# Zero-filled rows and columns for the products of layer 2 of a four-layer convolution and scan network

## Chip, cores and metric

The kernel runs on one core of a Trainium2 chip. The metric is the device time of one execution in microseconds (us). Several executions were timed, and the median is compared. A profile of one execution was taken with the hardware profiler; all its times count from the start of its span.

## The reference, cut to what matters

The network takes four images of 64 channels and 64 x 64 pixels, all float32, through four layers. Layers 0 and 3 are state-space scans with convolutions and a norm around them, and layer 1 is a larger scan in two directions. The change is in layer 2. As the kernel carries it out, layer 2 computes this for every pixel:

- a 3 x 3 convolution from 64 to 32 channels, with a bias;
- a leaky rectifier, the larger of `0.2 * h` and `h`;
- a 1 x 1 convolution from 32 channels to 9 values, with a bias, and a softmax over the 9 values, which gives a 3 x 3 filter of its own for each pixel;
- the filtered image: the sum over the 9 neighbours of filter value times pixel, the same filter for all 64 channels;
- twice the pixel minus the filtered image, which goes to layer 3.

## The kernel before, in words

`image` runs the four layers one after the other for each of the four images. A compile-time scheduler orders the instructions of each engine; each engine then runs its own list in order and waits for semaphores. Only layer 1 has its order written out by hand (`in_order`). In layer 2 the list is what the scheduler makes of the calls at the end of `layer2` (L1066 to L1071): `weights(c + 1)` is issued ahead of `filtered(c)`, and `turned(c + 1)` behind it.

The image lies in `x2` with a border of zeros, twice: the upper half of the rows is read from partitions 0 to 63 (the channels), and a copy made at L984 puts the lower half on partitions 64 to 127. So one chunk `c` covers 512 pixels of the upper half and 512 of the lower half, and there are four chunks per image.

For each chunk:

- `weights` makes the filters. For each of the 9 taps and each half it issues one product (L1008, recorded at the helper line L158): 64 rows of the array (the channels of that half), 32 columns (the hidden channels), 512 moving columns (pixels). The two halves use different rows and different columns of the array and write partitions 0 to 31 and 32 to 63 of `p1`. ScalarE adds the bias (L1013, tile `h1` of 64 x 512), and VectorE applies the rectifier (L1014). Four second products (L1017) take `h1` as the stationary side, 64 rows by 128 pixels, with the 18 columns of `l2_w2` moving. VectorE and ScalarE make the softmax (L1024 to L1033).
- `turned` transposes the filters (L1040), so that 18 rows (two halves of 9 taps) by 512 pixels result, and ScalarE copies them from PSUM to `wT` (L1045).
- `filtered` spreads each tap. For tap k a product with the one-hot matrix `pick[:, k]` (18 rows, 128 columns) and `wT` (18 rows, 512 moving columns) copies the filter value of a pixel to all 64 channels of its half, into `pk` (L1056, four PSUM buffers). VectorE multiplies `pk` by the shifted image to `m` (L1058, four buffers), and GpSimd subtracts `m` from the accumulator `acc` (L1060, for eight taps). The accumulator starts as twice the pixel (L1053). For the last tap GpSimd writes the result of each half to `x3` (L1064).

A float32 product is recorded as two matmuls and two weight loads. One 3 x 3 convolution of a chunk is thus 36 records, in 18 pairs of one record for each half, and the nine spreads are 18 records.

Layer 3 begins with `mamba_front`: the products `d_pc` and `d_pz` (64 rows, 128 columns) read `x3`, and the copy `d_xb` (L394) fills a constant. `setup` loads all constants once, those of layer 2 at L212 to L221, on the SyncE queue.

Of the kernel before, what the change touches and what calls it, by code (L numbers as in the profile page):

```python
# [10 lines left out]
F32 = mybir.dt.float32  # L11
AF = mybir.ActivationFunctionType
# [7 lines left out]
NB, C, H, W = 4, 64, 64, 64  # L20
HW = H * W
TOK = 512
# [43 lines left out]
class Net:  # L66
# [94 lines left out]
    def setup(self, sp, pp):  # L161
        nc = self.nc
        self.use_exp()
        self.unscale = self.ctile([128, 1], "unscale")
        nc.vector.memset(self.unscale, -23.0 * math.log(2.0))
        self.shift = self.ctile([128, 1], "shift")
        nc.vector.memset(self.shift, -SHIFT)
        self.ln_half = self.ctile([128, 1], "ln_half")
        nc.vector.memset(self.ln_half, -math.log(2.0))
        self.ln_eps = self.ctile([128, 1], "ln_eps")  # L170
        nc.vector.memset(self.ln_eps, LN_EPS)
        self.ident = ident = self.ctile([128, 128], "ident")
        make_identity(nc, ident)


        self.tri_in = ti = self.ctile([128, 128], "tri_in")
        nc.gpsimd.memset(ti, 1.0)
        nc.gpsimd.affine_select(
            out=ti, in_=ti, compare_op=ALU.is_ge, fill=0.0, base=0,
            pattern=[[1, 128]], channel_multiplier=-1,  # L180
        )
        nc.gpsimd.memset(ti[0:64, 64:128], 0.0)
        self.tri_after = ta = self.ctile([128, 128], "tri_after")
        nc.gpsimd.memset(ta, 1.0)
        nc.gpsimd.affine_select(
            out=ta, in_=ta, compare_op=ALU.is_ge, fill=0.0, base=-1,
            pattern=[[-1, 128]], channel_multiplier=1,
        )
        nc.gpsimd.memset(ta[64:128, 0:64], 0.0)

        self.tri2 = t2 = self.ctile([128, 64], "tri2")
        nc.vector.tensor_tensor(t2, ti[:, 0:64], ti[:, 64:128], ALU.add)
        self.ident2 = i2 = self.ctile([128, 64], "ident2")
        nc.vector.tensor_tensor(i2, ident[:, 0:64], ident[:, 64:128], ALU.add)
        nc.vector.tensor_scalar(i2, i2, math.exp(SHIFT - LN_EPS), None, ALU.mult)

        self.mask48 = m48 = self.ctile([64 + GC, GC], "mask48")
        nc.vector.tensor_tensor(
            m48, ident[0 : 64 + GC, 0:GC], ident[0 : 64 + GC, 64 : 64 + GC], ALU.add
        )  # L200

        self.mean64 = self.ctile([C, C], "mean64")
        nc.vector.memset(self.mean64, 1.0 / C)
        self.cen64 = self.ctile([C, C], "cen64")
        nc.vector.tensor_tensor(self.cen64, ident[0:C, 0:C], self.mean64, ALU.subtract)

        self.setup_l0(sp, pp)
        self.l1 = [self.setup_l1(sp, pp, d) for d in "wh"]
        self.l1_beta = self.ctile([C, 1], "l1_beta")
        nc.vector.tensor_tensor(self.l1_beta, self.l1[0]["beta"], self.l1[1]["beta"], ALU.add)  # L210

        self.l2_w1 = self.ctile([2 * C, 9, 32], "l2_w1")  # L212
        self.l2_b1 = self.ctile([C, 1], "l2_b1")
        self.l2_w2 = self.ctile([C, 2, 9], "l2_w2")
        nc.vector.memset(self.l2_w2, 0.0)
        self.l2_b2 = self.ctile([128, 9], "l2_b2")
        nc.sync.dma_start(self.l2_b2, self.a["l2_b2"].to_broadcast([128, 9]))
        for h in range(2):
            nc.sync.dma_start(self.l2_w1[h * C : (h + 1) * C], self.a["l2_w1"])
            nc.sync.dma_start(self.l2_b1[32 * h : 32 * h + 32], self.a["l2_b1"])  # L220
            nc.sync.dma_start(self.l2_w2[32 * h : 32 * h + 32, h], self.a["l2_w2"])  # L221
        self.setup_l3(sp, pp)

    def bn_scale(self, out_s, out_b, g, b, m, v):
# [753 lines left out]
    def layer2(self, b, x2):  # L978


        nc, tc = self.nc, self.tc
# [3 lines left out]
        with ExitStack() as ctx:  # L985
            sp = ctx.enter_context(tc.tile_pool(name=f"c{b}_s", bufs=2))
            ps = ctx.enter_context(tc.tile_pool(name=f"c{b}_ps", bufs=4, space=PSUM))
            pb = ctx.enter_context(tc.tile_pool(name=f"c{b}_pb", bufs=4, space=PSUM))
            rows = lambda x: x.rearrange("p (r w) -> p r w", w=W)
            pick = sp.tile([18, 9, 2 * C], F32, name=f"pick{b}", tag="pick", bufs=1)  # L990
            for h in range(2):
                nc.vector.tensor_copy(
                    pick[:, :, h * C : (h + 1) * C],
                    self.ident[0:18, 9 * h : 9 * h + 9].unsqueeze(2).to_broadcast([18, 9, C]),
                )

            def view(c, k):
                r = c * ROWS + k // 3
                return x2[:, r : r + ROWS, k % 3 : k % 3 + W]

            def weights(c):

                n = f"c{b}_{c}"
                p1 = ps.tile([128, TOK], F32, name=f"{n}_p1", tag="ps")
                for k in range(9):
                    for h in range(2):
                        P = slice(h * C, (h + 1) * C)
                        self.mm(  # L1008
                            p1[32 * h : 32 * h + 32], self.l2_w1[P, k, :], view(c, k)[P],
                            k == 0, k == 8,  # L1010
                        )
                h1 = sp.tile([C, TOK], F32, name=f"{n}_h1", tag="h1")
                nc.scalar.activation(h1, p1[0:C], AF.Identity, bias=self.l2_b1)  # L1013
                nc.vector.scalar_tensor_tensor(h1, h1, 0.2, h1, ALU.mult, ALU.max)  # L1014
                p2 = ps.tile([128, TOK], F32, name=f"{n}_p2", tag="ps")
                for j in range(4):
                    self.mm(  # L1017
                        p2[:, 18 * j : 18 * j + 18], h1[:, 128 * j : 128 * j + 128],
                        self.l2_w2.rearrange("p h k -> p (h k)"),
                    )  # L1020
                wl = sp.tile([128, 8, 9], F32, name=f"{n}_wl", tag="wl")
                st = sp.tile([128, 8], F32, name=f"{n}_st", tag="st")
                wide = st.unsqueeze(2).to_broadcast([128, 8, 9])
                nc.vector.tensor_tensor(  # L1024
                    wl, p2[:, 0:72].rearrange("p (j k) -> p j k", k=9),
                    self.l2_b2.unsqueeze(1).to_broadcast([128, 8, 9]), ALU.add,
                )
                nc.vector.tensor_reduce(st, wl, AX.X, ALU.max)
                nc.vector.tensor_tensor(wl, wl, wide, ALU.subtract)
                nc.scalar.activation(wl, wl, AF.Exp)  # L1030
                nc.vector.tensor_reduce(st, wl, AX.X, ALU.add)
                nc.vector.reciprocal(st, st)
                nc.vector.tensor_tensor(wl, wl, wide, ALU.mult)  # L1033
                return wl

            def turned(c, wl):
                n = f"c{b}_{c}"
                p3 = ps.tile([128, TOK], F32, name=f"{n}_p3", tag="ps")
                for j in range(4):
                    nc.tensor.transpose(  # L1040
                        p3[0:18, 128 * j : 128 * j + 128],
                        wl[:, 2 * j : 2 * j + 2, :].rearrange("p h k -> p (h k)"), self.ident,
                    )
                wT = sp.tile([18, TOK], F32, name=f"{n}_wT", tag="wT")
                nc.scalar.copy(wT, p3[0:18])  # L1045
                return wT

            def filtered(c, wT):
# [12 lines left out]
                for h in range(2):  # L1061
                    P = slice(h * C, (h + 1) * C)
                    t0 = 3 + c * TOK + h * HW // 2
                    nc.gpsimd.tensor_tensor(x3[:, t0 : t0 + TOK], acc[P], m[P], ALU.subtract)  # L1064

            wT = turned(0, weights(0))  # L1066
            for c in range(NCH // 2):
                wl = weights(c + 1) if c + 1 < NCH // 2 else None
                filtered(c, wT)
                if wl is not None:  # L1070
                    wT = turned(c + 1, wl)  # L1071
# [80 lines left out]
```

## Time and profile before

| | |
|---|---|
| median of 3 runs | 20212.52 us (20205.84 to 20241.59) |
| profiled execution, its own time | 20241.61 us |
| its span in the profile | 20239.9 us |
| mean granted TensorE clock | 0.952 |
| layer 2 of the first image, first convolution record to the last write of `x3` | 4470.6 to about 4581.1 us |
| the 3 x 3 convolutions start in the other images at | 9509.1, 14564.8 and 19610.1 us |

The profile lists for each group of instructions the source line, the engine, the operation, the tile written and the tiles read, the shape and the number of records. `PE` is TensorE's matmul and `PEld` its weight load; `DVE` is VectorE, `ACT` ScalarE, `POOL` GpSimd and `SP` SyncE. `18*128 18x512` on a matmul means 18 rows and 128 columns of the array and 512 moving columns. Tile names are given with the numbers left out: `c_p` stands for p1, p2 and p3 of layer 2, `c_pk` for the spread filters, `c_m` for the products on VectorE, `c_acc` for the accumulator, `c_h` for h1; names with `d_` belong to layer 3, and `x` written at L1064 is `x3`. The granted clock is the share of TensorE's full clock that its throttle let through. Matmuls are pipelined and a record's length holds its latency, so the pace of a stream is read from the distance between starts.

### The profile page before, as it was taken

To read this page: it belongs to the slowest core of one execution; us is meant where nothing else is said; L and a number is where in the kernel's file an instruction comes from. 1 tells how busy PE (TensorE), PEld (TensorE's weight loads), DVE (VectorE), ACT (ScalarE), POOL (GpSimd) and SP (SyncE) were. 2 spreads that over 40 slices of the span, in tenths; PEclk is the share of its full clock that TensorE was granted. 3 is DMA by queue.
4 is the path that set the end of the run, shared out by engine and by line. 5 is a ranking of instruction groups with operands and counts; after the bars stand their busy time and mean duration, and the time that the engine had idled before them with its cause. 6 is when DMAs were issued, how large, how long until landed. Compare 5 with 4: busy or idle time off the path is not lost. (4 is left out here: it accounts for less than half of the span.)

```text
span 20239.9 us, 622630 instructions
## 1 busy us (share of the span) xinstructions
PE 18436.4 (91%) x269256; PEld 11821.8 (58%) x269256; DVE 16728.8 (83%) x20282; ACT 12294.7 (61%) x15342; POOL 10582.6 (52%) x8660
## 2 busy tenths in 40 slices
PE   7899999997799999999789999999977999999997
PEld 2666666662266666666226666666622666666652
DVE  7888878878888888887988888888798888788879
ACT  3577667763367766775336776777533677667753
POOL 4555545555555555555555554555555555455555
PEclk9999999998899999999889999999988999999998
DMA  0233333320023333332002333333200233333320
GB/s 6 64 82 82 81 77 81 81 70 4 1 67 83 83 77 80 81 82 66 4 1 70 83 82 75 81 81 82 65 4 1 72 83 82 75 81 81 83 63 2
DMA packets 558931, 1264.96 MB, mean 62 GB/s; under 512 B 159416, under 2 KB 160800, under 8 KB 556192
## 3 DMA queue, kind: packets, MB, share of 16 engines
q1 hardware_dynamic: 556192, 1225.12, 24.6%
q8 instruction: 2124, 34.80, 0.7%
q14 instruction: 615, 5.04, 0.1%
HBM read 6.24 MB, written 4.19 MB: 1 GB/s over the span
## 5 line engine op out<-in xcount | busy, mean ns | idle before, releaser
L857 ACT ACTIVATE b_k_e<-b_z,shift 128x768 f32<-128x768 f32 x6144 | 5532.2, 900 | 4474.7 <-PE b_z L158 3718.5
L865 POOL TENSOR_TENSOR b_k_tB<-b_BC,tri 128x512 f32<-128x512 f32 x3072 | 3437.7, 1119 | 7431.7 <-PE b_u_S L158 6664.8
L903 DVE TENSOR_TENSOR b_k_r<-b_u_S,b_k_r 128x768 f32<-128x768 f32 x6144 | 5860.2, 954 | 977.6 <-DMA b_k_r<-b_k_r 262.2
L880 DVE TENSOR_TENSOR b_k_e<-b_k_e,b_wt 128x768 f32<-128x768 f32 x6144 | 6176.4, 1005 | 29.2 <-ACT b_k_e L857 29.2
L158 PE MATMUL b_u_S<-b_k_e,b_k_tB 64*64 64x192 f32 x98304 | 5425.8, 335 | 583.8 <-DVE b_k_r L903 491.8
L857 ACT ACTIVATE b_k_r<-b_z,ln_eps 128x768 f32<-128x768 f32 x6144 | 5488.7, 893 | 0.0
L158 PE MATMUL b_y<-b_k_r,b_k_dC 64*64 64x192 f32 x98304 | 5192.2, 323 | 64.0 <-ACT b_yt L923 61.3
L158 PE MATMUL b_z<-A,b_T 48*64 48x384 f32 x49152 | 5215.4, 487 | 4.3 <-ACT b_k_r L857 4.1
L158 PEld LDWEIGHTS b_y<-b_k_r,b_k_dC 64*64 64x64 f32 x98304 | 3915.9, 133 | 2171.8 <-issue 1489.2
L865 POOL TENSOR_TENSOR b_k_dC<-b_BC,ident 128x512 f32<-128x512 f32 x3072 | 4755.9, 1548 | 3.3 <-DMA b_BC<-b_BC 1.9
L158 PEld LDWEIGHTS b_u_S<-b_k_e,b_k_tB 64*64 64x64 f32 x98304 | 3278.3, 132 | 1851.9 <-DVE b_k_r L903 1015.2
L158 PEld LDWEIGHTS b_z<-A,b_T 48*64 48x64 f32 x49152 | 1913.5, 134 | 225.5 <-DVE b_yg L772 57.8
L438 ACT ACTIVATE d_a<-d_dl,l_A 128x512 f32<-128x512 f32 x512 | 368.7, 721 | 1089.8 <-DVE d_h L443 1089.8
L438 ACT ACTIVATE a_a<-a_dl,l_A 128x512 f32<-128x512 f32 x512 | 367.9, 720 | 1052.1 <-DVE a_h L443 911.6
L447 POOL TENSOR_TENSOR a_y<-a_y,a_o 128x512 f32<-128x512 f32 x512 | 821.1, 1604 | 287.9 <-DVE a_o L446 274.0
L447 POOL TENSOR_TENSOR d_y<-d_y,d_o 128x512 f32<-128x512 f32 x512 | 758.8, 1482 | 221.8 <-DVE d_o L446 208.5
L158 PE MATMUL a_pq<-a_sl,a_xb 128*128 128x512 f32 x1024 | 626.2, 696 | 262.1 <-DVE a_o L446 151.7
L158 PE MATMUL d_pq<-d_sl,d_xb 128*128 128x512 f32 x1024 | 643.9, 715 | 232.3 <-DVE d_o L446 185.1
L158 PE MATMUL d_pb<-d_sl,d_xb 128*128 128x512 f32 x1024 | 650.3, 722 | 180.8 <-DVE d_o L446 177.6
L443 DVE TENSOR_TENSOR_SCAN d_h<-d_a,l_state,d_g 128x512 f32<-128x512 f32 x512 | 738.2, 1458 | 5.4
L443 DVE TENSOR_TENSOR_SCAN a_h<-a_a,l_state,a_g 128x512 f32<-128x512 f32 x512 | 697.9, 1365 | 17.2 <-ACT a_a L438 9.8
L158 PE MATMUL a_pb<-a_sl,a_xb 128*128 128x512 f32 x1024 | 605.9, 677 | 41.2 <-DVE a_o L446 38.1
(343 smaller groups left out, 12651.5 us busy)
## 6 DMA issues: line engine op xcount, KB each, us to landing
b_k_r<-b_k_r SPq DMA_DIRECT2D x6144, 192.0 KB, 3.0
b_BC<-b_BC SPq DMA_DIRECT2D x512, 12.0 KB, 1.9
xin<-in_x SPq DMA_DIRECT2D x16, 256.0 KB, 6.0
out<-d_so SPq DMA_DIRECT2D x32, 128.0 KB, 2.3
l1w_cw<-in_l1w_cw SPq DMA_DIRECT2D x1, 192.0 KB, 3.3
l1h_cw<-in_l1h_cw SPq DMA_DIRECT2D x1, 192.0 KB
t_l1w_in<-in_l1w_in SPq DMA_DIRECT2D x1, 144.0 KB, 2.2
t_l1w_xbc<-in_l1w_xbc SPq DMA_DIRECT2D x1, 144.0 KB
```

What stands on the lines that cost most here:

```text
L158: self.nc.tensor.matmul(out, lhsT=lhsT, rhs=rhs, start=start, stop=stop)
L438: nc.scalar.activation(a, dl, AF.Exp, scale=m["A"][:, i : i + 1])
L443: nc.vector.tensor_tensor_scan(h, a, g, st, ALU.mult, ALU.add)
L447: nc.gpsimd.tensor_tensor(y, y, o, ALU.add)
L857: nc.scalar.activation(o.rearrange("p x (j c) -> p j x c", j=2), zin, AF.Sigmoid, bias=bias, scale=scale)
L865: nc.gpsimd.tensor_tensor(out, m.unsqueeze(3).to_broadcast(shape), x.unsqueeze(1).unsqueeze(2).to_broadcast(shape), ALU.mult,)
L880: nc.vector.tensor_tensor(e, e, chunks[q]["w"][:, i, :].unsqueeze(1).unsqueeze(2).to_broadcast([128, 2, 2, D1]), ALU.mult,)
L903: nc.vector.tensor_tensor(r, S[k][:, :, 0:UC], r, ALU.mult)
```

## The change

Every product of layer 2 that left rows or columns of the array unused, the transposes apart, is extended with zeros:

- The spread: `pick` has 128 rows in place of 18 (built from 128 rows of the identity, so rows 18 to 127 are zero). The moving side comes from a new tile `turns` of 128 partitions by two chunks, set to zero once per image on GpSimd; the copy at L1045 writes its first 18 rows. `turns` replaces the two buffers of `wT`.
- The convolution: `l2_w1` has 64 columns per half, of which the last 32 are zero, so the halves write partitions 0 to 63 and 64 to 127 of `p1`.
- The second product: `h1` and `l2_w2` have 128 partitions, those of the unused hidden channels zero. ScalarE's and VectorE's steps on `h1` cover 128 x 512.
- In `setup` the three constants are set to zero on VectorE ahead of their loads, and each load fills part of its tile.

```diff
-        self.l2_w1 = self.ctile([2 * C, 9, 32], "l2_w1")
-        self.l2_b1 = self.ctile([C, 1], "l2_b1")
-        self.l2_w2 = self.ctile([C, 2, 9], "l2_w2")
-        nc.vector.memset(self.l2_w2, 0.0)
+        self.l2_w1 = self.ctile([2 * C, 9, C], "l2_w1")
+        self.l2_b1 = self.ctile([2 * C, 1], "l2_b1")
+        self.l2_w2 = self.ctile([2 * C, 2, 9], "l2_w2")
+        for t in (self.l2_w1, self.l2_b1, self.l2_w2):
+            nc.vector.memset(t, 0.0)
...
-            nc.sync.dma_start(self.l2_w1[h * C : (h + 1) * C], self.a["l2_w1"])
-            nc.sync.dma_start(self.l2_b1[32 * h : 32 * h + 32], self.a["l2_b1"])
-            nc.sync.dma_start(self.l2_w2[32 * h : 32 * h + 32, h], self.a["l2_w2"])
+            nc.sync.dma_start(self.l2_w1[h * C : (h + 1) * C, :, 0:32], self.a["l2_w1"])
+            nc.sync.dma_start(self.l2_b1[h * C : h * C + 32], self.a["l2_b1"])
+            nc.sync.dma_start(self.l2_w2[h * C : h * C + 32, h], self.a["l2_w2"])
...
-            pick = sp.tile([18, 9, 2 * C], F32, name=f"pick{b}", tag="pick", bufs=1)
+            pick = sp.tile([128, 9, 2 * C], F32, name=f"pick{b}", tag="pick", bufs=1)
             for h in range(2):
                 nc.vector.tensor_copy(
                     pick[:, :, h * C : (h + 1) * C],
-                    self.ident[0:18, 9 * h : 9 * h + 9].unsqueeze(2).to_broadcast([18, 9, C]),
+                    self.ident[:, 9 * h : 9 * h + 9].unsqueeze(2).to_broadcast([128, 9, C]),
                 )
+            turns = sp.tile([128, 2, TOK], F32, name=f"turns{b}", tag="turns", bufs=1)
+            nc.gpsimd.memset(turns, 0.0)
...
                         self.mm(
-                            p1[32 * h : 32 * h + 32], self.l2_w1[P, k, :], view(c, k)[P],
-                            k == 0, k == 8,
+                            p1[P], self.l2_w1[P, k, :], view(c, k)[P], k == 0, k == 8,
                         )
-                h1 = sp.tile([C, TOK], F32, name=f"{n}_h1", tag="h1")
-                nc.scalar.activation(h1, p1[0:C], AF.Identity, bias=self.l2_b1)
+                h1 = sp.tile([128, TOK], F32, name=f"{n}_h1", tag="h1")
+                nc.scalar.activation(h1, p1, AF.Identity, bias=self.l2_b1)
...
-                wT = sp.tile([18, TOK], F32, name=f"{n}_wT", tag="wT")
-                nc.scalar.copy(wT, p3[0:18])
+                wT = turns[:, c % 2, :]
+                nc.scalar.copy(wT[0:18], p3[0:18])
                 return wT
```

## Prediction, made before the changed kernel was run

> **What bounds the kernel now.** I read the page first, then layer 2 alone: its clock in stretches of 2 us, its groups by tile, and its order of time.
>
> ```profile
> span 20239.9 us, 622630 instructions
> PE 18436.4 (91%) x269256; PEld 11821.8 (58%) x269256; DVE 16728.8 (83%) x20282; ACT 12294.7 (61%) x15342; POOL 10582.6 (52%) x8660
> PEclk9999999998899999999889999999988999999998
> ```
>
> TensorE is the busiest engine over the span. Its granted clock dips where each image leaves layer 1. Layer 2 lies there: 4470.6 to 4581.1 us in the first image, 110 us, some 442 us or 2.2% in all. Its clock, from the stretches (columns: from:to, length, PE busy, clock, DMA):
>
> ```profile
> 4496.00:4498.00 2.00, 2.00 (x7) 1.00 0.00 0
> 4498.00:4500.00 2.00, 2.00 (x11) 1.00 0.00 0
> 4500.00:4502.00 2.00, 2.00 (x4) 0.55 0.00 0
> 4510.00:4512.00 2.00, 2.00 (x6) 0.50 0.00 0
> 4514.00:4516.00 2.00, 2.00 (x8) 0.50 0.00 0
> 4518.00:4520.00 2.00, 2.00 (x12) 1.00 0.00 0
> 4598.00:4600.00 2.00, 2.00 (x4) 0.50 0.00 0
> 4606.00:4608.00 2.00, 2.00 (x3) 0.50 0.00 0
> 4610.00:4612.00 2.00, 2.00 (x6) 1.00 0.00 0
> ```
>
> TensorE is always busy here, yet its clock halves. The spreads of chunk 0 start at 4496.67; 4 us later the clock is at 0.5. The next convolution starts at 4512.20 and has it back by 4518.
>
> ```profile
> L158 PE MATMUL c_p<-x,l_w x576: 587/588/1059, 4470.6 to 19687.6; 64*32 64x512 f32 x192
> L158 PE MATMUL c_pk<-c_wT,pick x288: 587/1052/1217, 4496.7 to 19717.8; 18*128 18x512 f32 x144
> ```
>
> Fastest, median and slowest (ns): a spread costs 587 at full clock and 1052 mostly. By starts, a record takes 0.43 us warm and 0.853 cold.
>
> ```profile
> 4512.20 10.41 PE L158 MATMUL c_p<-x,l_w 64*32 64x512 f32 x36
> 4522.54 1.98 PE L158 MATMUL c_pk<-c_wT,pick 18*128 18x512 f32 x4
> 4524.45 1.06 PE L158 MATMUL c_p<-l_w,c_h 64*128 64x18 f32 x8
> 4525.44 10.32 PE L158 MATMUL c_pk<-c_wT,pick 18*128 18x512 f32 x14
> 4535.69 1.02 PE L1040 MATMUL c_p<-ident,c_wl 128*18 128x128 f32 x4
> 4536.64 10.13 PE L158 MATMUL c_p<-x,l_w 64*32 64x512 f32 x36
> ```
>
> One chunk on TensorE (start, length): no gap between the groups, so its order sets layer 2's pace. GpSimd, next in line, waits 8.33 us before chunk 1's first subtraction.
>
> **Which products hold the clock?** Layer 3's `d_pc`/`d_pz` (64 rows, 128 columns, one after the other) keep TensorE full from 4596.96 to 4605.8 at 0.50. `d_pb`/`d_pq` (128*128) follow at 4605.79 and have 1.00 by 4610. The convolution, two concurrent products of 64 rows by 32 columns, also regains it. It uses fewer cells of the array (4096) than `d_pc` (8192), but 128 rows. So rows in use decide here, not cells and not busy time; 18 and 64 are too few.
>
> **What the Trainium skill says.** (1) "TensorE: Matmul & The Clock Gate", Part 1: a monitor of TensorE's activity passes half the clock pulses or all, judged over a window of about 3.4 us. The trace agrees on the halves and the delay (4 us above). The page calls the measure busy-ness; the trace shows 2.00 of 2.00 us busy at 0.50, so the trace decides. (2) Same part, on the peak-current limiter: it depends on data, zeros do not trip it. That is another throttle, but it makes "zero rows do not count" a fair rival. (3) "TensorEngine Tiling (Array Packing)", Key Properties: tiles work independently, in parallel. Agreed: 36 convolution records at about 0.214 us each, half the 0.43 us of one alone. (4) "TensorE: Matmul & The Clock Gate", LDWEIGHTS (loading the stationary operand): loading goes by columns, not rows. Agreed: 18*128 loads take 181 ns at best, 64*128 loads 182.
>
> **The change, part by part,** on the span of 20239.9 us (20241.6 with what lies around it; 29.1 above the median).
>
> *Spread on 128 rows.* Unknown: does a zero row count as a row in use? Bounds: 0.43 us a record if so (the spread's own warm pace, and `d_pb`'s on 128*128), 0.853 if not. I take 0.43: every case above sorts by the rows that the instruction names, and layer 1's `b_z`, whose moving side is a diagonal times a column, and `b_y`, with a diagonal weight, leave the clock near 1 (0.98 from 500 to 4400), though never alone. The period from spread to spread, per chunk: first two spreads 1.91, second product 1.00, seven spreads 14 x 0.43 = 6.0 (before 10.25), transposes 0.95, convolution 18 pairs x 0.43 = 7.7 (before 10.06, its first pairs cold): 17.6 us, before 24.2. Chunk 2 ends without a convolution, but with 0.75 us for the copy of `wT`: 10.6. First spread of chunk 0 to first of chunk 3: 17.6 + 17.6 + 10.6 = 45.8 us. Before: 65.2, 65.35, 64.9, 65.1 in the four images. **Saved: 19.3 us each.**
>
> *What is late next: GpSimd.* Its first subtraction starts 2.2 us after the first spread, its second 4.0 after it (VectorE takes softmax steps between). Then they follow every 1.35 us (six took 8.03): 4.0 + 7 x 1.35 = 13.4, two final writes 2.6, next start value 1.57: 17.6 us. The next chunk wants it at 17.6 + 2.2, so it has 2 us to spare. In chunk 3 it hasn't: spreads begin at 10.6, GpSimd is free at 17.6. Eight subtractions of 1.35 and 2.6 for the writes: `x3` is done 31.0 us after chunk 2's first spread, 20.4 after chunk 3's; before 19.2. VectorE's last product needs the buffer that the fifth subtraction frees (17.6 + 6.75 = 24.4, plus 0.8): 25.2, or 14.6 after chunk 3's first spread. `d_pc` waits for that product (the trace names it as what ended its wait); before, it started 16.6 us after chunk 3's first spread, so 2.0 later. **Layer 3 starts 19.3 + 2.0 = 21.3 us earlier.** `d_xb` waits for `x3`: it ends 20.4 + 5.8 - 14.6 = 11.6 us after `d_pc`'s start; VectorE's next step came 12.8 after it. So it stays hidden, with 1.2 us of cover. The clock at `d_pc` stays 0.5, as TensorE waits for GpSimd just before.
>
> *Convolution on 64 columns.* Records and moving columns stay. Loads grow from 106 ns to some 132 (64*64 in layer 1), two per 0.43 us pair, and overlap. Taken as nothing; the other end is a rival.
>
> *Second product, rectifier, bias.* Length goes by the free size: 0. *Zeroing `turns`.* 128 x 1024; 128 x 4489 took 3.83, so about 0.9 us per image, in a GpSimd wait of 18.7 us ahead of L1053; without it 0.9 x 4. *`pick`.* Same free size; 0.
>
> *Setup.* VectorE's memset of 128 x 576 (some 0.6 us after 0.22 for 192) falls into its wait of 1.26 us for the first load. The two strided loads of `l2_w1`, 576 pieces of 128 bytes each, stand in SyncE's queue ahead of layer 3's constants and `xin`: 0 to 3 us, once; taken 1.
>
> **Sum:** 4 x 21.3 - 1 = 84 us. From the median: 20212.5 - 84 = **20128 us** (0.42%).
>
> **Rivals,** with their chances. *Zero rows don't count (16 in 100).* Then every record keeps 0.853 us, and the changed kernel does what it says for nothing: 20212 + 1, near 20213. For: the current limiter's example; no stage here streams zero rows alone. Against: the sorting by rows. *The clock holds only in part (7 in 100).* The second product (1.0 us, few moving columns) and the transposes with their copy interrupt the stream; if each costs a window, about half is lost: 20212.5 - 42 = 20170. Against: layer 3 keeps 1.00 from 4610 to 4616 with TensorE at half load. *Slower: the halves stop running together (4 in 100).* At 64 columns a half would wait for the other's. Then each convolution is 36 records of 64 rows one by one, as cold as `d_pc`: 36 x 0.853 = 30.7 in place of 7.7, 23 us x 16 chunks = 368, less 84: 20212 + 284 = 20496. It decides once a pair costs 84 / 288 = 0.29 us more than 0.43. Against: layer 1's 64*64 products run four at a time: 16 records of 192 columns in 0.88 us.
>
> **How the numbers follow.** The likeliest case has 73 in 100: 20128, from 20090 (layer 3's first products warm too, 4.5 us x 4, and runs as spread as before, some 20 either way) to 20165. Going up to 20190 takes in the partial case; the unmoved clock and the slow case, 20 in 100, stay out. A measurement of this kernel tells about 0.2% (40 us) from no change. Faster by more: 73 and half of the partial case, 0.76. Same: 16 and the other half, 0.20. Slower: 0.04.
>
> **What would show it.** Right: spreads near 590 ns in the median; clock 1.00 from the first spread of chunk 0 to the end of chunk 2; 17.6 us from chunk to chunk; GpSimd without a gap in chunk 3; `d_pc` 86.6 us after layer 2's first convolution record (107.9 before). Wrong: spreads at 1052 (zero rows don't count); convolution pairs beyond 0.43 us with a clock of 1; the clock falling after the second product; `d_xb` ahead of a waiting step of layer 3.

## The result

| | before | changed |
|---|---|---|
| median | 20221.96 us (6 runs, 20202.9 to 20241.59) | 20120.89 us (6 runs, 20106.55 to 20147.73) |
| profiled execution | 20241.61 us, span 20239.9 us | 20117.56 us, span 20115.8 us |
| mean granted TensorE clock | 0.952 | 0.959 |
| first convolution record of layer 2 to first `d_pc`, four images | 107.9, 107.7, 109.6, 109.6 us | 85.5, 84.3, 84.8, 84.8 us |

The ratio is 0.9952 (95% interval 0.9939 to 0.9965), so the kernel is 97 us faster (71 to 123); the two medians of the table differ by 101 us. The forecast was 20128 us, from 20090 to 20190, counted from the 20212.5 us of the first three runs.

The clock of the changed kernel in the first image's layer 2, in the same stretches of 2 us as before (from:to, length, TensorE busy, clock, DMA):

```profile
4482.00:4484.00 2.00, 2.00 (x8) 1.00 0.00 0
4500.00:4502.00 2.00, 2.00 (x10) 1.00 0.00 0
4520.00:4522.00 2.00, 2.00 (x6) 1.00 0.00 0
4540.00:4542.00 2.00, 1.95 (x3) 0.65 0.00 0
4542.00:4544.00 2.00, 2.00 (x4) 0.50 0.00 0
```

Spreads begin at 4482.49, and the clock is 1.00 from there until layer 3's first products of 64 rows, at 4540.05. The groups by tile (fastest, median, slowest in ns) say the same for all four images:

```profile
L158 PE MATMUL c_p<-x,l_w x576: 587/588/1113, 4454.5 to 19571.9; 64*64 64x512 f32 x192
L158 PE MATMUL c_pk<-turns,pick x288: 592/592/697, 4482.5 to 19590.9; 128*128 128x512 f32 x144
```

The median spread was 1052 ns; now the slowest is 697. One chunk on TensorE, and the end of the layer (start, length):

```profile
4499.61 1.98 PE L158 MATMUL c_pk<-turns,pick 128*128 128x512 f32 x4
4501.43 0.96 PE L158 MATMUL c_p<-l_w,c_h 128*128 128x18 f32 x8
4502.24 6.25 PE L158 MATMUL c_pk<-turns,pick 128*128 128x512 f32 x14
4508.34 0.60 PE L1042 MATMUL c_p<-ident,c_wl 128*18 128x128 f32 x4
4508.87 7.94 PE L158 MATMUL c_p<-x,l_w 64*64 64x512 f32 x36
4516.74 1.98 PE L158 MATMUL c_pk<-turns,pick 128*128 128x512 f32 x4
...
4526.78 6.28 PE L158 MATMUL c_pk<-turns,pick 128*128 128x512 f32 x14 [0.72 <-ACT turns L1047]
4533.33 1.12 PE L158 MATMUL c_pk<-turns,pick 128*128 128x512 f32 x2 [0.27 <-DVE c_m L1060]
...
4540.05 6.68 PE L158 MATMUL d_pc<-x,l_wk 64*128 64x512 f32 x8 [4.25 <-DVE c_m L1060]
```

From chunk to chunk it is 17.13 us in place of 24.2 to 25.9. In the last chunk TensorE waits, and at its end 4.25 us, for VectorE's products. One of these products in the last chunk, before and changed:

```profile
4567.46 0.69 DVE L1058 TENSOR_TENSOR c_m<-c_pk,x 128x512 f32<-128x512 f32 x1 [1.01 <-PE c_pk L158]
```

```profile
4535.28 0.69 DVE L1060 TENSOR_TENSOR c_m<-c_pk,x 128x512 f32<-128x512 f32 x1 [0.66 <-POOL c_acc L1062]
```

Before, VectorE waited for a spread; now it waits for GpSimd, which holds the buffers of `m` (run 6 tries this). GpSimd in the last two chunks:

```profile
4520.54 9.35 POOL L1062 TENSOR_TENSOR c_acc<-c_acc,c_m 128x512 f32<-128x512 f32 x7 [0.17 <-DVE c_st L1030]
4529.97 2.58 POOL L1066 TENSOR_TENSOR x<-c_acc,c_m 64x512 f32<-64x512 f32 x2
4532.63 10.67 POOL L1062 TENSOR_TENSOR c_acc<-c_acc,c_m 128x512 f32<-128x512 f32 x8
4543.37 2.57 POOL L1066 TENSOR_TENSOR x<-c_acc,c_m 64x512 f32<-64x512 f32 x2
```

It has no gap from 4520.54 to the end at 4545.94: the engine that sets the end of the layer is another than before.

**Where the time went, by layers.** I took the starts of four products from each trace: the first `b_z` (layer 1 begins), the first convolution record of layer 2, the first `d_pc`, and the last `d_po` (layer 3 ends). Sums of the four images in us; layer 0 holds the setup too.

| kernel | layer 0 | layer 1 | layer 2 | layer 3 |
|---|---|---|---|---|
| before | 2296.1 | 15481.1 | 434.8 | 2010.5 |
| changed | 2279.3 | 15468.8 | 339.4 | 2011.0 |
| changed, second profile (run 8) | 2253.8 | 15463.9 | 340.0 | 2011.1 |
| changed, third profile (run 9) | 2267.4 | 15464.9 | 338.3 | 2011.3 |

Layer 2 gives 95.4 us, nearly the 97 of the ratio. The two spans differ by 124; the other 29 are layers 0 and 1, and three profiles of one and the same kernel differ by 25 us in layer 0, so these 29 are not put down to the change.

### The profile page after: what moved, and what is told of

It reads as the page before. It is cut to its first block, busy times and chain, and to the rows that moved or that the text cites. A ratio compares the mean times of both kernels' runs of the same rounds, so it can differ in the third digit from the quotient of the medians.

```text
span 20115.8 us, 622640 instructions
## 1 busy us (share of the span) xinstructions
PE 18292.8 (91%) x269256; PEld 11796.2 (59%) x269256; DVE 16734.8 (83%) x20284; ACT 12292.4 (61%) x15342; POOL 10587.7 (53%) x8664
## 5 line engine op out<-in xcount | busy, mean ns | idle before, releaser
L158 PE MATMUL a_pb<-a_sl,a_xb 128*128 128x512 f32 x1024 | 599.1, 670 | 42.4 <-DVE a_o L447 39.0
```

Of the source, the lines that this page charges most:

```text
L158: self.nc.tensor.matmul(out, lhsT=lhsT, rhs=rhs, start=start, stop=stop)
```

## The experiments

My theory: the clock is granted by the rows of the array that the running products name; the spreads with their 18 rows lost it, and 128 named rows keep it, zeros or not. The rivals: the filling of the other products does it (or their changes of shape); the measure is gradual; the data count.

**1. The spread alone.** The changed kernel with the convolution, the second product and their constants as before:

```diff
-        self.l2_w1 = self.ctile([2 * C, 9, C], "l2_w1")
+        self.l2_w1 = self.ctile([2 * C, 9, 32], "l2_w1")
...
-                            p1[P], self.l2_w1[P, k, :], view(c, k)[P], k == 0, k == 8,
+                            p1[32 * h : 32 * h + 32], self.l2_w1[P, k, :], view(c, k)[P],
+                            k == 0, k == 8,
...
-                nc.scalar.activation(h1, p1, AF.Identity, bias=self.l2_b1)
+                nc.scalar.activation(h1, p1[0:C], AF.Identity, bias=self.l2_b1)
```

> Only the spread is filled to 128 rows; convolution (32 columns per half), bias, rectifier and second product (64 rows) are as before. My theory, that the rows of the spread decide the clock: the whole gain, a ratio of 0.995 to the kernel before (0.9940 to 0.9965), spreads at a median of 592 ns, clock 1.00 from the first spread of chunk 0 to chunk 3, some 17 us from chunk to chunk. Rival, that the array must be filled in every product of the layer (or that the changes of tile shape between the products cost): half the gain or less, 0.9975 or more, and the clock falling in or behind the convolutions.

Measured: 20156.66 us, 0.9968 (0.9955 to 0.9980). The spreads are at 592 ns, chunks follow each other every 17.4 us, and layer 2 sums to 343.6 us.

```profile
4518.78 1.98 PE L158 MATMUL c_pk<-turns,pick 128*128 128x512 f32 x4
4520.70 1.06 PE L158 MATMUL c_p<-l_w,c_h 64*128 64x18 f32 x8
4521.69 6.28 PE L158 MATMUL c_pk<-turns,pick 128*128 128x512 f32 x14
```

So 91 of the 95 us of layer 2 are the spread's. Most of the rest shows in these lines: at a clock of 1.00 the second product with 64 rows lasts 0.99 us from its start to that of the next spreads, in place of 0.81 with 128 rows in the changed kernel, and the two spreads ahead of it 1.92 in place of 1.82. By total this run was slower than layer 2 lets one expect, just outside the range (0.9965); run 9 comes back to it.

**2. The convolution and the second product alone.** The kernel before with the other part of the change (the diff of run 1 turned round).

> Only the convolution (64 columns per half), bias, rectifier and second product (128 rows) are filled; the spread has 18 rows as before. Theory: no gain, ratio 1.000 (0.9985 to 1.0015), spreads at a median of 1052 ns, clock 0.50 in the spreads, some 24 to 26 us from chunk to chunk; the second product may save 0.1 us per chunk where it falls into a stretch at full clock. Rival (fill everywhere): a gain of 0.1 to 0.3%.

Measured: 20238.11 us, 1.0003 (0.9996 to 1.0009), layer 2 at 437.5 us (434.8 before). The spreads:

```profile
L158 PEld LDWEIGHTS c_pk<-c_wT,pick x288: 181/328/333, 4474.6 to 19713.3; 18*128 18x128 f32 x144
L158 PE MATMUL c_pk<-c_wT,pick x288: 587/1056/1215, 4474.6 to 19714.1; 18*128 18x512 f32 x144
```

In the median, loads and matmuls of 18 rows stay as slow as at half the clock. Filling the other products gives nothing by itself.

**3. How many rows?** The changed kernel, the spreads naming another number of rows in each image; `turns` and `pick` are unchanged.

```diff
+            K = (32, 64, 96, 112)[b]
...
-                    self.mm(pk, pick[:, k], wT)
+                    self.mm(pk, pick[0:K, k], wT[0:K])
```

> The changed kernel, but the spread products name 32 rows in the first image, 64 in the second, 96 in the third and 112 in the fourth. Theory: what counts is the rows named, and the limit lies above 64. So the first two images have the clock at 0.50 in their spreads and take 24 to 26 us from chunk to chunk, the fourth has 1.00 and 17.1 us; the third is open, and one of the two. Rival, a measure that grows with the rows: a clock between 0.5 and 1 on average, moving from window to window, that rises from image to image.

Measured, in one profile (20210.16 us): layer 2 takes 108.5 and 108.6 us in the first two images, 84.8 and 83.9 in the others. From the first spread of a chunk to that of the next it is 24.2 to 25.9 us with 32 rows and 24.2 with 64, as before with 18 rows, and 17.13 us with 96 and with 112. The same group of seven spreads with 64 and with 96 rows, and then the clock in a stretch inside it, for all four images:

```profile
9543.31 11.58 PE L158 MATMUL c_pk<-turns,pick 64*128 64x512 f32 x14
...
14614.87 6.25 PE L158 MATMUL c_pk<-turns,pick 96*128 96x512 f32 x14
```

```profile
4499.00:4510.00 11.00, 11.00 (x14) 0.51 0.00 0
9544.00:9555.00 11.00, 11.00 (x15) 0.50 0.00 0
14615.00:14621.00 6.00, 6.00 (x16) 1.00 0.00 1
19634.00:19640.00 6.00, 6.00 (x20) 1.00 0.01 1
```

TensorE is fully busy in all four (second number of each line), and the clock is either half or whole. The clock goes by a step and no slope here, and 64 rows are below it.

**4. Ones in place of zeros.** In images 2 and 4 the unused rows of the moving side hold ones; the weights there stay zero.

```diff
-            nc.gpsimd.memset(turns, 0.0)
+            nc.gpsimd.memset(turns, (0.0, 1.0, 0.0, 1.0)[b])
```

> The changed kernel, but in the second and fourth image the unused 110 rows of the moving side hold ones in place of zeros (the weights there stay zero, so the sums are the same). Theory: the data don't matter, all four images have spreads of 592 ns at a clock of 1.00 and 17.1 us from chunk to chunk. Rival, that moving data count and zeros are just above a limit: the images with ones would hold the clock longer behind the last spread or differ in their records from those with zeros.

Measured (one profile, 20097.71 us): spreads 592/592/697 ns over all images, layer 2 at 85.6, 84.2, 84.2, 83.5 us. Images with ones (the second and fourth) and with zeros don't differ beyond what one kernel shows from image to image. The weights of the added rows are zero in all four, so products other than zero in these rows were not tried.

**5. Where is the step?** As run 3, with `K = (65, 72, 80, 88)[b]`.

> The changed kernel, the spread products naming 65, 72, 80 and 88 rows in the four images (64 were too few, 96 enough). If rows are counted in groups of 32 that a product touches, all four have three groups as 96 does and hold the clock: 17.1 us from chunk to chunk in every image. If single rows are counted, the low ones fall to 0.50 (24 us) and a later image shows the limit.

Measured (one profile, 20129.71 us): layer 2 takes 85.8, 85.4, 85.5, 84.4 us. All spreads of the four images (fastest, median, slowest in ns):

```profile
L158 PE MATMUL c_pk<-turns,pick x288: 592/592/697, 4496.9 to 19602.5; 65*128 65x512 f32 x36, 72*128 72x512 f32 x36, 80*128 80x512 f32 x36, 88*128 88x512 f32 x36
```

The clock is 1.00 in the first image too, from 4498 to 4546 us, with 65 rows. One row more than 64 is worth the whole gain. That fits a count of groups of 32 rows, of which 65 touches a third, and as well a limit in single rows right above 64; these runs don't part the two, nor any other rule that has 64 rows on one side and 65 on the other.

**6. Is GpSimd what is late in the last chunk?** The changed kernel, with the last chunk's start value, subtractions and writes on VectorE, behind its products, and nine buffers of `m`.

```diff
+                last = c == NCH // 2 - 1
+                eng = nc.vector if last else nc.gpsimd
+                ms = []
...
-                    m = sp.tile([2 * C, TOK], F32, name=f"{n}_m{k}", tag="m", bufs=4)
+                    m = sp.tile([2 * C, TOK], F32, name=f"{n}_m{k}", tag="m", bufs=9)
...
-                    if k < 8:
+                    if last:
+                        ms.append(m)
+                    elif k < 8:
                         nc.gpsimd.tensor_tensor(acc, acc, m, ALU.subtract)
+                for x in ms[:8]:
+                    nc.vector.tensor_tensor(acc, acc, x, ALU.subtract)
...
```

> The changed kernel, with the subtractions of the last chunk of each image on VectorE in place of GpSimd (issued behind its nine products) and nine buffers of m in place of four. Theory, that GpSimd's unfinished chunk 2 is what is late in chunk 3: the last product on VectorE ends some 9.8 us after chunk 3's first spread in place of 13.2, layer 3's first product starts 3.5 us earlier in each image (some 81.3 us from the first convolution record to it, 84.8 in the changed kernel), and the sum is some 14 us or 0.07%, less than the total shows. Rival, that TensorE or the constant copy d_xb sets layer 3's start: 84.8 us stay, or VectorE's step behind d_xb starts no earlier.

Measured: 20100.27 us, 0.9941 (0.9929 to 0.9954), beside 0.9942 for the changed kernel in the same rounds. Layer 2 takes 81.8, 81.6, 81.8, 81.5 us, 326.7 in sum, 12.7 less than in the changed kernel's first profile.

```profile
4535.07 7.15 PE L158 MATMUL c_pk<-turns,pick 128*128 128x512 f32 x16 [0.72 <-ACT turns L1047]
...
4545.38 6.61 PE L158 MATMUL d_pc<-x,l_wk 64*128 64x512 f32 x8 [1.87 <-DVE c_m L1063]
```

`d_pc` starts 10.3 us after the last chunk's first spread, in place of 13.3, and its wait falls from 4.25 to 1.87 us. So GpSimd was what came late. The run changes two things at once, the buffers and the engine, so it doesn't tell which of them frees VectorE; either takes GpSimd out of its way. `d_xb` doesn't set the pace: VectorE's step behind it starts 12.2 us after `d_pc`, 12.3 in the changed kernel, so it moves forward with it. By total the 13 us can't be told from scatter.

**7. The same filling in layers 0 and 3.** If named rows decide, the products of 64 rows there should gain too. Their weights (`wk`, `wz`, `l0_wt`) and inputs (`xin`, `hn`, `x3`) get 128 partitions, the added ones zero; three of the edits:

```diff
-        m["wk"] = wk = self.ctile([C, 4, DIN], f"{n}_wk")
+        m["wk"] = wk = self.ctile([2 * C, 4, DIN], f"{n}_wk")
+        nc.vector.memset(wk, 0.0)
...
-            nc.gpsimd.memset(hn[:, 0:3], 0.0)
+            nc.gpsimd.memset(hn[0:C, 0:3], 0.0)
+            nc.gpsimd.memset(hn[C:], 0.0)
...
-        x3 = self.xp.tile([C, HW + 3], F32, name=f"x3_{b}", tag="xb")
+        x3w = self.xp.tile([2 * C, HW + 3], F32, name=f"x3_{b}", tag="xb")
+        x3 = x3w[0:C]
+        nc.gpsimd.memset(x3w[C:], 0.0)
```

> The changed kernel, with the same filling where layers 0 and 3 begin a chunk: their products of 64 rows (a_px, a_pc, a_pz, d_pc, d_pz) name 128 rows, the added weights and inputs zero, set on GpSimd once per image. Theory, that rows named decide the clock wherever TensorE is full: layer 3's first products keep 1.00 (8.9 us become some 4.5), no stretch at 0.50 remains in which TensorE is full, and the mean clock rises from 0.959 to 0.975 or more. In time, VectorE's waits for TensorE in the changed kernel, 36 us in layer 0 of the first image and 10 in its layer 3, bound the gain at 180 us; I expect some 50 us against the changed kernel (20 to 90). Rival, that VectorE bounds these layers: the clock rises and the time stays within 20 us.

Measured: 20015.05 us, 0.9899 (0.9883 to 0.9914). That is 90 us below the changed kernel's 20105.54 in the same rounds (run 8). Beside that kernel's profile, layer 0 is 42.4 us shorter (2211.4), layer 3 23.0 us (1988.1), layers 1 and 2 nearly as before. The two profiles differ by 69 us and not by 90, mostly because the profiled execution of the changed kernel was 18 us below its median. So VectorE doesn't hide TensorE's cold stretches here, and the rival falls; the gain is larger than my 50 us. The second chunk's `d_pc` in the first image, in the changed kernel and here:

```profile
4558.06 7.19 PE L158 MATMUL d_pc<-x,l_wk 64*128 64x512 f32 x8
```

```profile
4543.07 5.77 PE L158 MATMUL d_pc<-x,l_wk 128*128 128x512 f32 x8
```

The expectation that no full stretch at half clock remains was wrong. From 4543 to 4550 TensorE is full at a mean clock of 0.68, since the clock is still at half from the wait before it and is regained only on the way; the mean over the run is 0.964, not 0.975. With `d_pz` the stretch takes 6.5 us, where the changed kernel takes 8.8 and some 4.5 were expected.

**8. The changed kernel once more,** in the same rounds as runs 6 and 7.

> The changed kernel itself, beside the others for comparison: ratio 0.9952 to the kernel before (0.9939 to 0.9965), layer 2 from first convolution record to layer 3's first product 84 to 86 us in each image.

Measured: 20105.54 us, 0.9942 (0.9930 to 0.9955); layer 2 at 83.8, 84.8, 85.6, 85.8 us.

**9. The spread alone again, beside the changed kernel.**

> The spread-only kernel once more, now on the same chip and in the same rounds as the changed kernel. In the first run its layer 2 lasted 343.6 us in the four images (changed kernel 339.5), but its total was 0.9968 of the kernel before, less than the 0.995 that follows from layer 2. If that was the scatter of layers 0 and 1, which the change doesn't touch, the total is 4 us above the changed kernel's, within some 20 us: 0.994 to 0.996. If the spread-only build runs layers 0 and 1 slower by itself, it stays near 0.9968, some 45 us above the changed kernel.

> The changed kernel beside the spread-only one: 0.9945 (0.993 to 0.9965).

Measured: the spread alone 20141.13 us, 0.9954 (0.9942 to 0.9967); the changed kernel 20111.76 us, 0.9941 (0.9928 to 0.9955). Layer 2: 342.5 and 338.3 us. The intervals overlap, but both times the spread alone came out higher by more than layer 2's 4 us: 36 us above the changed kernel's first median, and now 29. The profiles put it outside layer 2. Layer 0, where the order of instructions is the same, takes 2308.1 and 2293.2 us against 2279.3, 2253.8 and 2267.4 in the changed kernel; in the first profile layer 1 adds 28 us more (15497.0), in the second it adds nothing (15459.5). Other builds come as high: run 3 has 2296.6 us in layer 0 and the same 15497.0 in layer 1, run 2 2294.0 in layer 0. That speaks for scatter; a lasting effect of the build is not ruled out.

**10. Runs 6 and 7 together.**

> The fronts of layers 0 and 3 on 128 rows and the last chunk's subtractions on VectorE, together, on the changed kernel. Theory: the two gains add. The fronts alone took 0.9899 of the kernel before, the last chunk alone shortened layer 2 by 3.2 us in each image. So some 0.989 (0.9875 to 0.991), about 20000 us, with 81.5 us from the first convolution record to layer 3's first product and that product's stretch at a higher clock. Rival: with layer 3's first products faster, the constant copy d_xb or VectorE's longer list delays them, and no more than 0.9899 is reached.

Measured: 19983.82 us, 0.9887 (0.9870 to 0.9903), the fastest of all; layer 2 sums to 327.1 us, layer 3 to 1982.6, layer 0 to 2204.1. By layers the gains add. By total the step from run 7 (0.9899) is no larger than the intervals, so the total alone doesn't rule out the rival. This kernel beats the kernel before by 228 us, the changed kernel by 97 to 119 (0.9952 to 0.9941).

## Why the prediction was right, step by step

- **Which products hold the clock: right, and now shown.** The forecast sorted by the rows named, not by cells or busy time. Runs 3 and 5 vary this number alone, and the clock changes between 64 and 65 rows. The changed kernel's added rows hold zeros and its clock is 1.00, so "zero rows don't count" falls; run 4 adds that ones in the moving side give the same. The comparison of `d_pc` (64 rows, cold) with `d_pb` (128, warm) was what carried this step.
- **The period of a chunk: 17.6 forecast, 17.13 measured.** First two spreads 1.82 us (1.91), second product 0.81 (1.00), seven spreads 6.10 (6.0), transposes 0.53 (0.95), convolution 7.87 (7.7). The transposes were priced at what they cost before at half clock, though the forecast gives all this work the full clock. The second product ran at full clock before as well; its gain, and that of the two spreads ahead of it, comes with its own 128 rows, as run 1 keeps 0.99 and 1.92 us at a clock of 1.00. The forecast put that at nothing. From the first spread of chunk 0 to that of chunk 3 it is 44.3 us (45.8).
- **The clock through the breaks: right.** Neither the second product nor the transposes cost it, nor the wait of 4.25 us ahead of `d_pc`, so "holds only in part" falls. The argument against that rival was weaker than it read: of the 6 us with a clock of 1.00 in layer 3, TensorE was full in the first 2, and from 4616 to 4618 the clock was down to 0.56.
- **GpSimd late next: right in kind, 1.7 us too long.** It starts the last chunk's subtractions 15.9 us after chunk 2's first spread (17.6 forecast). The start value of 1.57 us that I put ahead of them was made a chunk earlier, at 4515.49. The profile of before had it so too: after 4539.36 no start value follows ahead of the last chunk. Eight subtractions take 10.67 us (10.8), the writes end 19.2 us after chunk 3's first spread (20.4), and `d_pc` starts 13.3 us after it (14.6). Run 6 shows the mechanism.
- **`d_xb` stays hidden: right, with less cover.** It starts 0.04 us after the last write of `x3`; VectorE's next step waits for ScalarE 0.61 us longer (1.2 forecast):

```profile
4545.98 5.78 DVE L395 COPY d_xb<-t_l_xbc 128x4096 f32<-128x4096 f32 x1 [5.98 <-POOL x L1066]
4552.37 1.22 DVE L110 SCALAR_TENSOR_TENSOR d_t<-d_v,d_t 128x1024 f32<-128x1024 f32 x1 [0.61 <-ACT d_t L109]
```

- **The clock at `d_pc`: a small miss.** I said it stays at 0.5; it was at 1.00 when `d_pc` began and fell within 0.6 us.
- **The edits at no cost: right.** Convolution pairs keep their pace of 0.44 us with 64 columns (7.87 us for 18 pairs, 7.85 with 32 columns in run 1), though a load grew from 106 to 133 ns, so the slow rival falls. On 128 partitions in place of 64, the bias step takes 687 ns (682 before) and the rectifier 692 (683). Zeroing `turns` takes 0.96 us at 4439.0, in a wait of GpSimd that still ends with the copy at L985. The setup put the first product of layer 0 from 36.60 to 36.96 us (36.65 and 36.86 in the other two profiles; 1 us taken).
- **The sum: 84 forecast, 95 measured in layer 2.** Per image 21.3 was forecast, and 22.4, 23.5, 24.8 and 24.8 came. In the first image the last chunk's start and the chunk's period gave 1.3 and 1.5 us more than forecast, and the first two convolutions, half cold before and after, took 1.9 more than in the profile of before (27.95 us to the first spread, 26.09 before); the latter goes one way or the other by image. That the time itself came within 7 us of the forecast is in part luck: the median of before rose by 9 us when the count went from three runs to six, and by gain the forecast is 13 to 17 us short.

## What to carry to other kernels

Where TensorE is fully busy and its granted clock still stands at half, look at how many rows of the array its products name, before you look for waits. Filling the contraction (the rows over which a product sums) with zero rows cost little here, where the instructions stay as many, and was worth nearly a factor of two on that stretch (0.43 us a record in place of 0.853). More columns brought nothing: run 2 has 64 in place of 32 in the convolution and keeps the time of before. Then work out which engine is late next: here GpSimd took back part of the gain in the last chunk.

## What was not expected of the hardware

- The step is sharp: spreads of 64 rows ran at a clock of 0.50 with TensorE busy for 11.00 of 11.00 us, spreads of 65 rows at 1.00. Two products of 64 rows that run together on different rows (the convolution) have the full clock as well.
- "TensorE: Matmul & The Clock Gate" of the Trainium skill, Part 1, explains the clock by how busy TensorE is. The halves and the delay are seen here, but the share of busy time was the same on both sides of the step (11.00 of 11.00 us at 0.50, 6.00 of 6.00 at 1.00 in run 3), so the measurement decides.
- Layer 0 of one and the same kernel takes 2254 to 2279 us in three profiles, and the time goes with the clock. Taking images 2 to 4 of all eleven profiles whose layer 0 is as before, those of 554.6 to 556.1 us have a mean clock of 0.844 to 0.857 in it, those of 561.1 to 564.3 us 0.825 to 0.843, and those of 570.1 to 580.2 us 0.794 to 0.820. With its products on 128 rows the clock is 0.87 to 0.88, and images 2 to 4 take 544 to 549 us each (run 7) and 544.0 to 544.2 us (run 10). So part of the scatter of the total seems to come from when these products find the clock at half; why that differs from one execution to the next was not tried.
